# A macaron block on one core: the second FFN's routing as a table of pieces beside the attention's end, with transposes by transfers

## The chip, the cores and the metric

The kernel runs on one core of one Trainium2 chip. The metric is the device time of one execution in microseconds; the figure shown for a kernel is the median of its runs. The engines are called PE (matmuls; PEld is its weight loads), DVE, ACT, POOL and SP, as the profile calls them. "L814" is line 814 of the kernel before.

## The reference

The input x has 2 batches of 4096 tokens with 512 features, in float32. Three steps each add to x:

- x = x + 0.5 FFN(layernorm(x))
- x = x + attention(layernorm(x))
- x = x + 0.5 FFN(layernorm(x)), with the same FFN weights as in the first step

The FFN routes every token to 64 slots. A hidden layer of 256 (exact gelu) gives 64 logits, the 8 largest are kept, and a softmax over these gives the token's weights alpha. Each slot's input is the alpha-weighted mean of all tokens, so the whole sequence has to be routed before the slots are updated. A recurrent cell (GRU) updates the slots, and the output of a token is its alpha times the new slot values, projected:

```
h = gelu(concat(x, slot_mean) @ w1.T + b1)
alpha = softmax over the top 8 of (h @ w2.T + b2) / (|tau| + 0.1)
slot_input = sum over t of alpha[t] * x[t];   slots = GRU(slot_input / sum of alpha, slots)
out = (alpha @ (slots @ wv.T + bv)) @ wo.T + bo
```

The attention is a linear one with a delta rule, in 16 heads of 32: q and k are normalised, a and b are sigmoids of projections, and a state of 32x32 per head runs over the tokens:

```
state = a * state + (b * (v - state @ k)) outer k;   y = state @ q
out = (rmsnorm(y) * g_norm * silu(x @ Wg)) @ Wo
```

## The kernel before, in words

The tokens are cut into 32 blocks of 128 positions, with both batches in one block (tile shapes carry NB = 2). Projections that need more than float16 precision are done as three float16 matmuls, from a high half and a low half of each operand (`mm3`, L127 to L130).

**The first FFN's routing** (`ffn_a_phase`, L309, called with "a") works in groups of 1, 4, ..., 4, 3 and 1 blocks. Every stage of a group is a generator with a start and an end on a common scale (PA, L1095), and `run_merged` (L60) merges them by due time. The stages: `a_load` brings x; `a_stats` (L355) takes mean and variance; `a_norm` (L368) writes the normalised tokens, casts them to the high half on ACT (L383), subtracts on POOL for the low half (L385), transposes both halves by 16 PE transposes a block into PSUM (L394) and copies them out, the high one on ACT (L397), the low one on DVE (L399); `a_hidden` (L402) does the hidden layer and the logits (L421); `a_topk` (L425) the top 8 and the weights; `a_slots` (L463) sums tokens into slots in one PSUM bank that stays open for the whole phase. Beside it the attention's weights are prepared: `split16` (L175) makes a high half on ACT and a low half on DVE. `gru` (L509) then updates the slots.

**The attention** (L647) is a software pipeline over the blocks. `PIPE` (L1097) is a table of words such as "prep.6": in each period k the generator of that stage for block k + 6 takes one step. One period handles one block, by stages of up to eight neighbouring blocks; its order is the order of every engine's queue (`run_pipe`, L75). `prep` (L781) adds the first FFN's output (`ffn_b`, L486), stores x1d, normalises, transposes the float32 block by four PE transposes for each batch (L814), casts to the high half on ACT (L816) and subtracts for the low half on DVE (L818). `qkproj` and `vgproj` project; `post` normalises q and k; `kk`, `dec`, `solve` make a triangular system and invert it on DVE; `chain` (L1000) carries the state over four chunks of the block; `tail` (L1056) applies gate, norm and output projection (L1080), adds x1 (L1083) and stores the block into x2d. The PSUM pool of the projections has three buffers, shared by the projections, by `prep`'s output of the FFN and by the tail.

**The second FFN** (`ffn_a_phase` with "c", L644) starts after the attention's pools are closed, so its first instructions wait for all of these. It loads x2d on SP (L602), keeps the last 12 blocks in SBUF (KEEP, L37), routes as the first one does, runs the recurrent cell, and then (`after_c`, L624) makes the output block by block (L641) and stores it.

Transfers issued by SP and ACT stand in these engines' instruction queues in program order. Pools allocated over freed memory wait for the whole of the pool that was there.

Of the kernel before, what the change touches and what calls it, by code (L numbers as in the profile page):

```python
# [19 lines left out]
P = 128  # L20
# [14 lines left out]
HEAD, TAIL = 1, 1  # L35
CFG = {"a": dict(XT=7, XN=2, XH=10), "c": dict(XT=4, XN=2, XH=11)}
KEEP = 12  # L37
F3A, F3X, F3L = 4, 11, 8
# [14 lines left out]
def split_blocks(n):  # L53

    cuts = [0] + list(range(HEAD, n - TAIL, GB)) + [n - TAIL, n]
    cuts = sorted(set(cuts))
    return [(a, b - a) for a, b in zip(cuts, cuts[1:])]
# [17 lines left out]
def run_pipe(tc, stages, n):  # L75


    order = []
    for w in PIPE.split():
        w, _, m = w.partition("*")  # L80
        name, lead = w.split(".")
        order += [(name, int(lead))] * int(m or 1)
    live = {}
    with tc.manual_schedule():
        for k in range(-max(lead for _, lead in order), n):
            for name, lead in order:
                t = k + lead
                if 0 <= t < n:
                    if (name, t) not in live:
                        live[name, t] = stages[name](t)  # L90
                    next(live[name, t], None)
# [3 lines left out]
def tile_macaron(  # L95
# [82 lines left out]

    isc1 = cp.tile([P, 1], F32, tag="isc1", name="isc1")
# [3 lines left out]
    aw = aw_es.enter_context(tc.tile_pool(name="aw", bufs=1))  # L183
    W = {}
    for n_, cols, dt in (("wqh", NQ, F16), ("wql", NQ, F16), ("wgh", 2 * D, F16), ("wgl", 2 * D, F16),
                         ("wo", D, F32)):
        W[n_] = aw.tile([P, KC, cols], dt, tag=n_, name=n_)
# [43 lines left out]
    def setup_gh(gp, big, ppj):  # L231
# [3 lines left out]
        whht = big.tile([P, KC, 3 * D], F32, tag="big", name="whht")  # L235
        for k in range(KC):
            nc.sync.dma_start(whht[:, k], whh[k * P:(k + 1) * P])
# [3 lines left out]
        nc.sync.dma_start(bsum, bhh.rearrange("(k p) -> p k", p=P))  # L241
        V.tensor_tensor(bsum[:, 0:8], bsum[:, 0:8], bihn[:, 0:8], ALU.add)
        ghb = gp.tile([P, 12, NS], F32, tag="ghb", name="ghbs")
        yield 0.1
        for g in range(12):
            pg = ppj.tile([P, NS], F32, tag="tr", name=f"pgh{g}")
            for k in range(KC):
                nc.tensor.matmul(pg, whht[:, k, g * P:(g + 1) * P], hsT[:, k], start=(k == 0), stop=(k == KC - 1))
            V.tensor_scalar(ghb[:, g], pg, bsum[:, g:g + 1], None, ALU.add)
            yield 0.1 + 0.9 * (g + 1) / 12  # L250
        nc.sync.dma_start(ghd, ghb)

    def setup_attention(gp, big, ppj):
# [5 lines left out]
        yield 0.1  # L259
        scales(gp, ppj, [s1[:, :, 0:2 * D], s1[:, :, 2 * D:]], scA[:, 0:2], iscA[:, 0:2], "wq")  # L260
        yield 0.3
        for k in range(KC):
            for s, i in ((slice(0, 2 * D), 0), (slice(2 * D, NQ), 1)):
                o = [W[n_][:, k, s] for n_ in ("wqh", "wql")]
                if i == 0:

                    o = [a.rearrange("p (q e g) -> p q g e", g=NG, e=C) for a in o]
                    src = s1[:, k, s].rearrange("p (q g e) -> p q g e", g=NG, e=C)
                    for g in range(NG):
                        split16(*(a[:, :, g] for a in o), src[:, :, g], scA[:, i:i + 1])  # L270
                else:
                    split16(*o, s1[:, k, s], scA[:, i:i + 1])
            yield 0.3 + 0.05 * (k + 1)
# [3 lines left out]
        yield 0.5  # L277
        scales(gp, ppj, [s2[:, :, 0:D], s2[:, :, D:]], scA[:, 2:4], iscA[:, 2:4], "wg")
        yield 0.7
        for k in range(KC):  # L280
            for i in range(2):
                s = slice(i * D, (i + 1) * D)
                split16(W["wgh"][:, k, s], W["wgl"][:, k, s], s2[:, k, s], scA[:, 2 + i:3 + i])
            yield 0.7 + 0.03 * (k + 1)
        gt = gp.tile([P, KC], F32, tag="gt", name="gt")
        nc.sync.dma_start(gt, gnorm.rearrange("(k p) -> p k", p=P))
        s3 = big.tile([P, KC, D], F32, tag="big", name="wo32")
        for k in range(KC):
            nc.sync.dma_start(s3[:, k], wo_a[k * P:(k + 1) * P])
        for k in range(KC):  # L290
            nc.scalar.mul(W["wo"][:, k], s3[:, k], gt[:, k:k + 1])
            yield 0.85 + 0.03 * (k + 1)
# [16 lines left out]
    def ffn_a_phase(load, adst, nm, extra, before=None, after=None):  # L309

        with tc.tile_pool(name=f"sl{nm}", bufs=1, space=PSUM) as slp, tc.tile_pool(name=f"gp{nm}", bufs=1) as gp:
            sl = slp.tile([P, KC, NB, NS], F32, tag="sl", name=f"sl{nm}")
            wacc = gp.tile([P, GB * NB, NS], F32, tag="wacc", name=f"wacc{nm}")
            gw = {}
            with tc.tile_pool(name=f"f{nm}", bufs=2) as wp, tc.tile_pool(name=f"fs{nm}", bufs=2) as sm, \
                    tc.tile_pool(name=f"ft{nm}", bufs=3, space=PSUM) as ptr, \
                    tc.tile_pool(name=f"fp{nm}", bufs=2, space=PSUM) as ppj, \
                    tc.tile_pool(name=f"fl{nm}", bufs=2, space=PSUM) as ppl:
                groups = split_blocks(NBLK)
                ng = len(groups)  # L320
                pools = (wp, sm, ptr, ppj, ppl)
                st = [dict() for _ in range(ng)]
                items = []
                for g, (b0, n) in enumerate(groups):
                    args = (st[g], nm, g, (b0, n), pools)
                    t0, t1 = b0 / GB, (b0 + n) / GB
                    items += [
# [840 lines left out]
```

## Time and profile before

| what | us |
|---|---|
| median of 3 runs | 2353.59 |
| lowest and highest run | 2349.47, 2361.57 |
| the profiled execution, its own time | 2342.8 |
| its span | 2341.0 |
| one attention period | 51.4 |

| stretch of the span, us | what runs there |
|---|---|
| 0 to 300 | first routing, preparing weights, recurrent cell |
| 300 to 468 | the attention's pipeline fills |
| 468 to 1959 | 29 periods of the attention |
| 1959 to 2004 | the last chain, the last tails |
| 2004 to 2250 | second routing |
| 2250 to 2341 | recurrent cell, output |

How to read it: the page gives each engine's busy time over the whole span, and the span in 40 slices of 58.5 us with the busy share in tenths, so that a 9 is 90% or more. Matmuls are pipelined and their ends are modelled, so that the busy time of PE is not its time at peak: where a price of PE is needed, the time from one start to the next is used. The views by stretch give, for each stretch, the busy time of every engine, the granted clock, and the share of the 16 DMA engines. A line of a group of instructions gives its line in the code, engine and operation, the tile written and the tiles read, the shapes and the count; then the busy time, the mean in ns, and the idle time before it with what ended it.

### The profile page before, as it was taken

The numbers are of one execution on the slowest core, as the hardware profiler recorded it, in microseconds if no ns is written. First come the engines' busy times: TensorE is split into PE (matmuls) and PEld (weight loads), VectorE is DVE, ScalarE is ACT, GpSimd is POOL, SyncE is SP. The second block draws the span as 40 slices with busy tenths as digits, with TensorE's granted clock in tenths as the row PEclk, the third lists the DMA queues.
The fourth block names the chain that finished last, engine by engine and source line by source line (L and its number), as shares of the span: only waits on it lengthen the run. The fifth ranks groups of instructions, "written<-read, shape, count | busy, mean of one in ns | idle before, by whom it ended". The sixth has DMA issues, their size and how long they took to land. (4 is left out here: it accounts for less than half of the span.)

```text
span 2341.0 us, 101047 instructions
## 1 busy us (share of the span) xinstructions
PE 2100.5 (90%) x44989; PEld 1585.4 (68%) x44989; DVE 1911.3 (82%) x4876; ACT 1148.9 (49%) x1957; POOL 808.5 (35%) x750
## 2 busy tenths in 40 slices
PE   5878878999999999999999999999999976588886
PEld 5767757767777676777767677777667754377774
DVE  7898538988888888888889888888888886489656
ACT  4677445544445444444545444554444421367631
POOL 2333114433334343333434333444333441134300
PEclk9898989999999999999999999999999988799997
DMA  6332323344443344343334444344444332630049
GB/s 212 123 127 91 96 87 129 119 133 130 142 134 126 123 136 132 128 150 121 126 124 139 128 136 148 120 127 132 135 128 146 102 97 70 219 110 29 2 149 368
DMA packets 176516, 302.75 MB, mean 129 GB/s; under 512 B 27984, under 2 KB 73552, under 8 KB 176080
## 3 DMA queue, kind: packets, MB, share of 16 engines
q1 hardware_dynamic: 161728, 256.45, 32.9%
q10 hardware_dynamic: 14352, 39.85, 5.2%
q8 instruction: 352, 5.77, 1.2%
q14 instruction: 84, 0.69, 0.1%
HBM read 189.23 MB, written 107.00 MB: 127 GB/s over the span
## 5 line engine op out<-in xcount | busy, mean ns | idle before, releaser
L1080 PE MATMUL apo<-wo,Gt 128*128 128x512 f32 x512 | 279.1, 630 | 24.5 <-DVE x1r L1083 24.5
L128 PE MATMUL pv<-xTh,wgh 128*128 128x256 f16 x1024 | 282.1, 275 | 0.0
L129 PE MATMUL pv<-xTh,wgl 128*128 128x256 f16 x1024 | 280.2, 274 | 0.1
L130 PE MATMUL pv<-xTl,wgh 128*128 128x256 f16 x1024 | 280.3, 274 | 0.0
L1014 POOL TENSOR_TENSOR ps<-ST,AC 128x256 f32<-128x256 f32 x128 | 105.5, 824 | 442.4 <-DVE ST L1038 442.4
L128 PE MATMUL pq<-wqh,xTh 128*128 128x384 f16 (+1 forms) x768 | 242.8, 316 | 1.5 <-issue 0.8
L129 PE MATMUL pq<-wqh,xTl 128*128 128x384 f16 (+1 forms) x768 | 240.9, 314 | 0.2 <-DVE xTl L818 0.2
L130 PE MATMUL pq<-wql,xTh 128*128 128x384 f16 (+1 forms) x768 | 240.7, 313 | 0.0
L862 POOL TENSOR_TENSOR qk<-qk,rn 128x512 f32<-128x512 f32 x128 | 137.6, 1075 | 231.7 <-issue 106.7
L836 ACT ACTIVATE qk<-pq,iscA 128x384 f32<-128x384 f32 (+1 forms) x192 | 105.4, 549 | 162.5 <-PE pq L130 139.5
L980 POOL TENSOR_TENSOR KQ<-KQ,Ax 128x512 f32<-128x512 f32 x128 | 168.4, 1315 | 0.4 <-PE pa L959 0.4
L764 DVE TENSOR_TENSOR tmp<-N,MT 128x256 f32<-128x256 f32 (+7 forms) x384 | 161.2, 426 | 5.6
L758 DVE TENSOR_TENSOR tmp<-N,U 128x256 f32<-128x256 f32 (+7 forms) x384 | 164.0, 434 | 1.4
L838 ACT ACTIVATE sq<-pq,iscA 128x384 f32<-128x384 f32 (+1 forms) x192 | 164.7, 858 | 0.0
L1018 PEld LDWEIGHTS pc<-KQ,S 32*32 32x32 f32 x8192 | 123.2, 106 | 50.6 <-ACT Y L1044 31.0
L760 DVE TENSOR_REDUCE MT<-tmp 128x32 f32<-128x256 f32 (+7 forms) x384 | 153.8, 407 | 0.0
L959 PE MATMUL pa<-KQ 32*32 32x64 f32 x8192 | 143.6, 217 | 11.2 <-ACT KQ L872 4.9
L1018 PE MATMUL pc<-KQ,S 32*32 32x64 f32 x8192 | 142.8, 217 | 9.5 <-DVE S L1040 4.9
L959 PEld LDWEIGHTS pa<-KQ 32*32 32x32 f32 x8192 | 121.7, 105 | 37.9 <-issue 14.9
L1035 PEld LDWEIGHTS pc<-X,u 32*32 32x32 f32 x8192 | 120.7, 105 | 38.6 <-issue 21.9
L1035 PE MATMUL pc<-X,u 32*32 32x64 f32 x8192 | 141.9, 216 | 5.2 <-ACT u L1032 3.7
L917 ACT ACTIVATE vg<-pv,iscA 128x512 f32<-128x512 f32 x128 | 88.1, 688 | 96.7 <-PE pv L130 88.7
(304 smaller groups left out, 5760.3 us busy)
## 6 DMA issues: line engine op xcount, KB each, us to landing
d<-a0d ACTq DMA_DIRECT2D x32, 528.0 KB
Ax<-a0d ACTq DMA_DIRECT2D x32, 528.0 KB
xt<-in_x_dram SPq DMA_DIRECT2D x32, 512.0 KB
x<-in_x_dram SPq DMA_DIRECT2D x64, 256.0 KB
x1d<-x SPq DMA_DIRECT2D x64, 256.0 KB
vtd<-vg SPq DMA_DIRECT2D x64, 256.0 KB
kd<-qk SPq DMA_DIRECT2D x64, 256.0 KB
XK<-kd SPq DMA_DIRECT2D x256, 64.0 KB
```

The source lines that it names most:

```text
L128: nc.tensor.matmul(po, lh, rh, start=start, stop=False, skip_group_check=True)
L129: nc.tensor.matmul(po, ll, rh, start=False, stop=False, skip_group_check=True)
L130: nc.tensor.matmul(po, lh, rl, start=False, stop=stop, skip_group_check=True)
L758: V.tensor_tensor(tv, vw(f, o10 + j0, [[C, n], [0, h], [1, ni]]), vw(U, ou + j0 * 17, [[0, n], [16, h], [1, ni]]), ALU.mult)
L760: yield lambda tv=tv, j0=j0: V.tensor_reduce(vw(mt, n * j0, [[1, n], [n, h]]), tv, AX.X, ALU.add)
L764: V.tensor_tensor(tv, vw(f, o11 + r0 * C, [[C, h], [0, n], [1, nk]]), vw(mt, 0, [[0, h], [n, n], [1, nk]]), ALU.mult)
L838: nc.scalar.activation(sq[:, f0:f1].rearrange("p (q g e) -> p q e g", g=NG, e=C), pq[:, 0:f1 - f0].rearrange("p (q e g) -> p q e g", g=NG, ...
L959: nc.tensor.matmul(pa[s, m], KQ[s, 0, c, b, g], KQ[s, :, c, b, g], start=(m == 0), stop=True, skip_group_check=True, tile_position=(32 * q ...
L980: nc.gpsimd.tensor_tensor(kc, kc, bass.AP(Ax.tensor, Ax[:, :, c].offset, [list(a[0]), [1, 2], list(a[1]), [1, C]]), ALU.mult)
L1018: nc.tensor.matmul(pcv[s, b, g, 0:2 * C], S[s, b, g], KQ[s, :, c, b, g], start=(g == 0), stop=False, skip_group_check=True, tile_position=tp)
L1035: nc.tensor.matmul(pcv[s, b, g, C:3 * C], u[s, b, g], d["X"][s, :, m], start=False, stop=True, skip_group_check=True, tile_position=tp)
L1080: nc.tensor.matmul(po, Gt[:, k, b], wo[:, k], start=(k == 0), stop=(k == KC - 1))
```

## The change

Four things are changed.

- **The second routing becomes a table of its own.** `ffn_a_phase` is cut into `route_open` and `route_close`; the stages yield at each small step; `ROUTE` is a table of words as PIPE is, with one period for a group of blocks, and the groups of the second FFN are 1, 3, 4, ..., 4, 3, 1. The logits are a stage of their own. `pieces` walks a table as a generator. The first FFN's routing still goes by due times (`merged`).
- **It is begun beside the attention's last three periods.** The attention's pools are split into an early and a late set. After the last step of any stage before the last four (vload, chain, tload, tail) the early set is closed, `open_c` opens the second routing's pools in that memory, and the routing's pieces are taken in proportion to the attention's until its period 0 has been done (AHEAD = 1.0). The x2 loads are issued by ACT. Pools wait by tile, not by pool (`reuse_waits="tile"`).
- **Token halves become feature-major by transposing transfers** (`dma_start_transpose`, on SP): in `prep` the block is cast to a high half and subtracted to a low half first, and both are transposed by transfers from SBUF to SBUF; in the second routing likewise. The first routing keeps its PE transposes.
- **Around it:** PIPE is written anew; the tail's and `prep`'s PSUM tiles move to a pool of one buffer (`ppo`) and the projections keep two; `setup_attention` splits weights by two ACT passes and a POOL subtraction (`split16p`) in finer steps; the normalised tokens overwrite the loaded ones except for kept blocks; buffer counts change (CFG, KEEP, F3X, F3L).

```diff
-CFG = {"a": dict(XT=7, XN=2, XH=10), "c": dict(XT=4, XN=2, XH=11)}
-KEEP = 12
-F3A, F3X, F3L = 4, 11, 8
+HEAD, TAIL = (1, 4), (4, 1)
+CFG = {"a": dict(XT=7, XH=9), "c": dict(XT=6, XH=8)}
+KEEP = 11
+AHEAD = 1.0
+F3A, F3X, F3L = 4, 12, 9
...
+def pieces(stages, n, table, extra=()):
...
+    for k in range(-max(lead for _, lead in order), n):
+        for e, (name, lead) in enumerate(order):
+            others(k + e / len(order))
+            t = k + lead
+            if 0 <= t < n:
+                if (name, t) not in live:
+                    live[name, t] = stages[name](t)
+                next(live[name, t], None)
+                yield k + (e + 1) / len(order)
+    others(n + 1)
...
+    def split16p(hi, lo, src, s):
+        nc.scalar.mul(src, src, s)
+        nc.scalar.copy(hi, src)
+        nc.gpsimd.tensor_tensor(lo, src, hi, ALU.subtract)
...
+    def route_open(nm, load, adst, extra, side):
...
+        ptr, ppj, ppl = (pool(fs, *a, space=PSUM) for a in (("ft", 3 if nm == "a" else 1), ("fp", 2), ("fl", 1)))
...
+    def a_norm(d, nm, g, pools):
...
             nc.scalar.copy(xh, xn)
+            yield
+            if nm == "a":
+                nc.gpsimd.tensor_tensor(xl, xn, xh, ALU.subtract)
...
+            else:
+                nc.sync.dma_start_transpose(xTh, flat(xh))
+                yield
+                nc.gpsimd.tensor_tensor(xl, xn, xh, ALU.subtract)
+                yield
+                nc.sync.dma_start_transpose(xTl, flat(xl))
+                yield
...
+    def load_x2(wp, t):
+        if t >= NBLK - KEEP:
+            xt = keep[t] = pk["xk"].tile([P, NB, D], F32, tag=f"x2_{t}", name=f"kx2_{t}")
+            xn = pk["xk"].tile([P, NB, D], F32, tag="xn", name=f"kxn{t}", bufs=2)
+        else:
+            xt = xn = wp.tile([P, NB, D], F32, tag="xt", name=f"xt2_{t}", bufs=CFG["c"]["XT"])
+        nc.scalar.dma_start(xt, x2d[t * P:(t + 1) * P])
+        return xt, xn
...
+    def open_c():
+        aw_es.close()
+        pk["ak"] = kp.enter_context(tc.tile_pool(name="ak", bufs=1, side="right", reuse_waits="tile")).tile(
+            [P, NBLK, NB, P], F16, tag="ak", name="ak")
+        pk["r"] = route_open("c", load_x2, alpha_keep, extra_c, "right")
+        return pieces(*pk["r"]["args"])
...
-        ppj = pool("a1p", 3, space=PSUM)
+        ppo = pool("a1o", 1, space=PSUM)
+        ppj = epool("a1p", 2, space=PSUM)
...
-                pt = ptr.tile([P, KC, P], F32, tag="tr", name=f"apt{t}_{b}")
-                for k in range(KC):
-                    nc.tensor.transpose(pt[:, k], xs[b][:, k * P:(k + 1) * P], ident)
-                yield
-                nc.scalar.copy(xTh[:, :, b], pt)
-                yield
-                V.tensor_tensor(xTl[:, :, b], pt, xTh[:, :, b], ALU.subtract)
+                xh = we.tile([P, D], F16, tag="xh", name=f"xh{t}_{b}", bufs=2)
+                nc.scalar.copy(xh, xs[b])
+                yield
+                nc.sync.dma_start_transpose(xTh[:, :, b], xh)
+                yield
+                xl = we.tile([P, D], F16, tag="xl", name=f"xl{t}_{b}", bufs=2)
+                V.tensor_tensor(xl, xs[b], xh, ALU.subtract)
+                yield
+                nc.sync.dma_start_transpose(xTl[:, :, b], xl)
                 yield
...
-        run_pipe(tc, stages, NBLK)
+        late = ("vload", "chain", "tload", "tail")
+        drain = NBLK - min(lead for name, lead in leads(PIPE) if name not in late)
+        rest = None
+        with tc.manual_schedule():
+            for now in pieces(stages, NBLK, PIPE):
+                if now >= drain and rest is None:
+                    ee.close()
+                    rest = open_c()
+                    at = next(rest)
+                    first = at
+                if rest is not None:
+                    while at < first + (AHEAD - first) * (now - drain) / (NBLK - drain):
+                        at = next(rest)
+    return rest
```

The new table of the routing:

```
ROUTE = """
    hid.2*2 topk.1*3 hid.2 load.4 topk.1 slots.0 topk.1*3 norm.2 topk.1 norm.2 stats.3 hid.2 norm.2 stats.3 topk.1 hid.2*3
    logit.2 stats.3*2 norm.2 hid.2 stats.3 norm.2 topk.1 hid.2 topk.1 hid.2 stats.3 norm.2 topk.1*2 hid.2*3 topk.1 logit.2
    hid.2 topk.1*2 norm.3 slots.1*4 norm.3 load.4 norm.3 slots.1*2 hid.2 slots.1 norm.3*2 slots.1 hid.2 norm.3*2 hid.2
    slots.1 norm.3*3 hid.2 norm.3*2 hid.2 topk.1 norm.3 stats.4 slots.1*2 stats.4 slots.1 hid.2 load.4 hid.2*2 logit.2
    norm.3*3 stats.4*2 norm.3 logit.2 slots.1 load.4 topk.2 hid.3 norm.3 slots.1 hid.3 topk.2*2 slots.1
"""
```

## The prediction

> **What bounds the kernel now.** I read four views in this order: the page (engine shares and slices), busy time by stretches, the waits of TensorE in the middle, and single rows where a price is needed. The page first.
>
> ```profile
> span 2341.0 us, 101047 instructions
> ...
> PE 2100.5 (90%) x44989; PEld 1585.4 (68%) x44989; DVE 1911.3 (82%) x4876; ACT 1148.9 (49%) x1957; POOL 808.5 (35%) x750
> ...
> PE   5878878999999999999999999999999976588886
> ...
> DVE  7898538988888888888889888888888886489656
> ```
>
> PE is at 9 only in the middle; both ends are lower, so the 90% is no statement about the ends. The stretches say where they are (columns: length, then busy us of PE, weight loads, DVE, ACT, POOL, granted clock, DMA share, GB/s).
>
> ```profile
> 468.00:1959.00 1491.00, 1435.61 (x36251) 1036.70 (x36249) 1302.73 (x3277) 700.62 (x1278) 579.49 (x582) 0.99 0.40 129
> 1959.00:2004.00 45.00, 30.80 (x738) 18.12 (x738) 11.12 (x22) 4.30 (x10) 3.83 (x5) 0.79 0.16 54
> 2004.00:2052.00 48.00, 26.02 (x237) 21.68 (x238) 28.40 (x73) 20.64 (x26) 11.60 (x7) 0.72 0.77 283
> 2052.00:2250.00 198.00, 165.75 (x2132) 147.35 (x2131) 156.56 (x455) 136.58 (x190) 71.77 (x39) 0.94 0.10 34
> 2250.00:2341.00 91.00, 63.29 (x280) 45.84 (x277) 54.51 (x108) 16.35 (x41) 0.00 (x0) 0.82 0.89 332
> ```
>
> I set the cuts. The last triangular solve ends at about 1959, and one attention period is 51.4 us (the same store of vtd is issued at 1009.69 and 1061.08), so 468 lies 29 periods earlier. In those 29 periods PE is busy 96%: the attention is bound by PE's work in order. From 1959 to 2004 the last chain and two tails run one after another, and DVE works 11 of 45 us. From 2004 the second routing starts cold: DVE 28 of 48 us, at a clock of 0.72. From 2052 to 2250 no engine is full (PE 84%, DVE 79%, ACT 69%). After 2250 the stores end last (DMA share 0.89).
>
> The seam at 2004 is a chain, seen in the timeline:
>
> ```profile
> 1999.21 0.32 SPq L1054 DMA_DIRECT2D x1r<-x1d  x1
> 2001.80 0.75 DVE L1083 SCALAR_TENSOR_TENSOR x1r<-apo,rms,x1r 128x512 f32<-128x512 f32 x1 [4.62 <-DMA x1r<-x1d]
> 2002.58 0.32 SPq L1085 DMA_DIRECT2D x2d<-x1r  x1
> 2004.76 0.52 POOL L460 MEMSET waccc<- 128x512 f32 x1 [15.07 <-DMA x2d<-x1r]
> 2004.76 3.28 SPq L602 DMA_DIRECT2D xt<-x2d  x4
> ```
>
> The routing's first load waits for the attention's very last store, though it reads block 0, stored 1500 us earlier; its first DVE instruction comes at 2012.05.
>
> **The change, part by part.** All sums are against the profiled execution, 2342.8 us (span 2341.0 and 1.8 around it); the median shown is 2353.59, 10.8 longer, and I move the result by that.
>
> *Attention's transposes.* Eight float32 transposes a period (L814) leave PE. Their busy time (272 ns each) overlaps, so I take the time until PE's next instruction starts:
>
> ```profile
> 1024.49 0.60 PE L814 MATMUL apt<-ident,x 128*128 128x128 f32 x4
> 1025.02 1.09 PE L1035 MATMUL pc<-X,u 32*32 32x64 f32 x64
> ...
> 1053.50 0.60 PE L814 MATMUL apt<-ident,x 128*128 128x128 f32 x4
> 1053.94 0.29 PE L128 MATMUL pq<-wqh,xTh 128*128 128x288 f16 x1
> ```
>
> 0.53 + 0.44 = 0.97 us a period. The copy and the subtraction remain, one on ACT (0.59) and one on DVE (0.68), now from SBUF. PE also waits:
>
> ```profile
> PE apo L1080 <- DVE x1r L1083: 20.4, 23, 1.8
> ```
>
> that is 0.85 us in each of some 24 periods. The new order and the tail's own PSUM bank could remove it, or add to it: one bank is now shared by the tail's sums, its two projections and prep's two, so each waits until DVE or ACT has read the last. I take no change in waits: 0.84 x 32 = -27 us, rounding 0.97 down for the first periods, which are not PE-bound. Bounds: 0.97 + 0.85 over 32 is -58; above, see the transfers.
>
> *Transposing transfers.* Four a period of 128 KB, 64 in the second routing of 256 KB, all on SP. No row of before has one. From below: the final stores move 379 GB/s (2300 to 2341), so 256 KB takes 0.7 us and 128 KB half of it. From above: the 161,728 packets of the main queue take 32.9% of 16 engines' 2341 us, 76 ns each; as rows of 256 bytes, 256 KB is 1024 packets, 4.9 us, and 128 KB 2.45 us. I take 1.5 and 0.75 us, nearer the lower end since most bytes here run near it, and a latency of 2.6 us as the plain load above (1999.21 to 2001.80). Counted in the new table, the last low half is issued 0.09 period, 4.5 us, before the projection that reads it, so 2.6 us is covered; where it is not, PE stops with all that stands behind. Each SP transfer also waits for ACT's or DVE's half, and behind it stand the kd and vtd stores and the XK loads, 0.3 to 2.4 us to issue each; DMA is 40% busy. Price if uncovered: 1 us a period is 32 us.
>
> *Second routing and drain.* 512 PE transposes, 32 ACT copies and 32 DVE copies go:
>
> ```profile
> L394 PE MATMUL fptc<-ident,xlc 128*128 128x128 f16 x256 | 31.6, 229 | 11.9 <-POOL xlc L385 11.9
> L394 PE MATMUL fptc<-ident,xhc 128*128 128x128 f16 x256 | 26.7, 225 | 20.9 <-ACT xhc L383 20.8
> L397 ACT COPY fxThc<-fptc 128x1024 f16<-128x1024 f16 x32 | 32.4, 1011 | 5.7 <-PE fptc L394 5.6
> L399 DVE COPY fxTlc<-fptc 128x1024 f16<-128x1024 f16 x32 | 21.7, 677 | 15.2 <-PE fptc L394 15.2
> ```
>
> From 2004 to 2250 that leaves PE 191.8 - 58.3 = 133.5, ACT 157.2 - 32.4 = 124.8, DVE 185.0 - 21.7 = 163.3 us: DVE is next. With the drain's own 11.1 it has 174 us of work between 1959 and the recurrent cell, and now all of it may overlap, since 11 blocks are normalised and 8 hidden beside the last chain and tails. At 85% full that is 205, and 10 for the last group's chain of logits, top-8 and slots (17 us at the end of before, part of it counted): 215 against 291, -76 us. Bounds of the filling: DVE's 79% of before gives 220 + 17 = 237, -54; its 97% between 100 and 200 us gives 180 + 10, -101. The chain's DVE steps now queue behind routing's (0.7 us each, up to 2.5 beside POOL); that is inside these ends. The x2 loads move to ACT's queue, where the chain's u and Y copies stand behind a load that waits for freed memory: at most the solve's lag, 5 us.
>
> *The first routing and setup.* 24 splits leave DVE (16 of 967 ns and 8 of 859, 22.4 us), ACT does each twice (852 and 720 ns more, 19.4 us), POOL subtracts (from 2.16 us per 1024 elements: 17.3 us). DVE is 97% busy there, ACT 75%: -5 us, between -15 and +10 (POOL beside DVE costs DVE time). The seam at 265 to 300, where waits go by tile, and the fill: -3, between -12 and +10, since prep's latency now has a transfer in it. The ending: one block more to load, 1.4 us, hidden or not: 0, between -10 and +5.
>
> Sum: -27 - 76 - 5 - 3 = -111. 2342.8 - 111 = 2232; against the median 2353.59 - 111 = **2243**.
>
> **A rule against it, and one for it.** No run here shows either. The Trainium skill, "VectorE: DVE Perf Modes", section "The three transpose paths", gives 1309 ns for a 128x128 block by DMA and 390 ns by TensorE; if eight blocks of a half queued up so, 64 halves would take 670 us, and the sum would be far slower than before. "Advanced Engine Details and Errata", section "X-Bar Transpose (TRN2)", calls such transfers as fast as ordinary ones at 350 to 400 GB/s; by that a half is 0.7 us and the sum stands.
>
> **The rivals.** (1) Forecast, 2243, own range 2195 to 2290, chance 0.53. (2) The overlap pays but the attention does not: the low halves land late behind XK loads (up to three of 0.55 to 2.4 us on SP) or the shared bank stops PE. At 1.6 us a period the 0.97 turns into +0.65, +21 instead of -27: 2291, chance 0.20. For: the one bank and 4.5 us of slack. Against: the tail's wait of 0.85 can go. (3) It doesn't do what it says: the begun routing cannot start since its memory is freed too late, or its pieces only lengthen the drain; then only DVE's copies count, -22 instead of -76: 2297, chance 0.08. (4) Slower: transposing transfers at 4.9 us a half. 64 halves take 314, with 25 to start 339 instead of 215, +124; in the attention two low and high halves in a row (2.45 each) miss the 4.5 us by some 2.5 with latency, +80: 2447. It decides from 64t + 25 = 215 + 111, t = 4.7 us a half, even if the attention is spared; chance 0.14. The rest, 0.05, is gains and losses that cancel.
>
> Faster by over 0.5% (about what a measurement of this kernel can tell from no change) is (1), (2) and most of (3): 0.80; within 0.06; slower 0.14. The range, 2190 to 2350, takes in the first three cases and leaves (4) out.
>
> **What would show it.** The period between equal stores falls to about 50.5 us; PE's wait for x1r stays under 1 us a period; no large wait of PE for a transfer into xTh or xTl; the 48 us gap of low DVE after the last store is gone; last store of x2d to the recurrent cell falls from 248 us to about 150. It is wrong if SP is seen waiting long behind a transpose, if a half lands over 4 us after issue, or if the drain grows by more than the 30 us that it takes from later.

## The result, and the profile after

The changed kernel takes 2431.1 us (median of 4 runs, 2419.34 to 2448.22) against 2354.99 us of before (4 runs, 2349.47 to 2361.57): ratio 1.0328, 95% interval 1.0256 to 1.0399. It is slower by 76 us; the forecast was 2243 and the range ended at 2350. The profiled execution of after took 2436.47 us with a span of 2434.7. Its page:

```profile
span 2434.7 us, 99970 instructions
...
PE 2098.8 (86%) x44221; PEld 1558.7 (64%) x44221; DVE 1891.1 (78%) x4816; ACT 1207.1 (50%) x2017; POOL 808.8 (33%) x778
...
PE   5787877889999999999999899999999996668775
...
DVE  7968545878888888878888788888888888366646
...
DMA packets 313873, 336.78 MB, mean 138 GB/s; under 512 B 165216, under 2 KB 210784, under 8 KB 313440
```

TensorE (PE) executes 768 matmuls fewer than before and is busy for about the same time, 2098.8 us against 2100.5; the count of packets under 512 bytes is 165216, where before has 27984:

```profile
DMA packets 176516, 302.75 MB, mean 129 GB/s; under 512 B 27984, under 2 KB 73552, under 8 KB 176080
```

The transposing transfers move 33.5 MB, and the trace's own packet records show them as rows of 256 bytes.

To find the loss I cut both profiled executions at the same four instructions: the first recurrent cell's first matmul (pw), the first and the last triangular solve (the DVE instruction that writes TT), and the second recurrent cell's first matmul. All kernels of this study, in us of their profiled executions, with the median time and its ratio to the kernel before, measured beside it:

| kernel | start to first cell | to first solve | first to last solve | to second cell | to the end | median | ratio [95%] |
|---|---|---|---|---|---|---|---|
| before | 273.9 | 132.5 | 1551.4 | 292.3 | 90.9 | 2354.99 | 1 |
| after | 291.5 | 143.8 | 1628.3 | 280.6 | 90.5 | 2431.10 | 1.0328 [1.0256, 1.0399] |
| attn_pe | 292.6 | 129.8 | 1518.7 | 279.1 | 90.9 | 2319.49 | 0.9829 [0.9800, 0.9859] |
| rout_pe | 294.8 | 146.0 | 1617.7 | 344.2 | 91.3 | 2495.49 | 1.0574 [1.0548, 1.0601] |
| both_pe | 294.2 | 129.8 | 1518.7 | 345.0 | 90.9 | 2378.38 | 1.0076 [1.0049, 1.0103] |
| attn_plain | 294.3 | 143.8 | 1680.6 | 276.8 | 92.4 | 2507.73 | 1.0601 [1.0546, 1.0656] |
| pe_oldsplit | 280.0 | 129.7 | 1515.9 | 270.6 | 91.0 | 2297.41 | 0.9747 [0.9721, 0.9774] |
| pe_dummy | 295.5 | 135.8 | 1620.9 | 276.8 | 89.6 | 2418.28 | 1.0261 [1.0243, 1.0280] |
| dummy_plain | 291.7 | 135.5 | 1511.1 | 281.4 | 91.1 | 2310.38 | 0.9797 [0.9774, 0.9819] |
| attn_none | 291.9 | 131.3 | 1499.5 | 274.1 | 90.9 | 2288.64 | 0.9716 [0.9694, 0.9738] |
| pe_late | 292.4 | 133.1 | 1519.2 | 265.5 | 90.2 | 2298.04 | 0.9743 [0.9715, 0.9770] |
| pe_mix | 293.5 | 130.8 | 1519.1 | 292.5 | 91.0 | 2328.71 | 0.9883 [0.9865, 0.9901] |
| pe_seq | 293.9 | 131.1 | 1515.3 | 296.1 | 90.9 | 2328.20 | 0.9895 [0.9854, 0.9937] |
| rout_none | 291.2 | 131.4 | 1518.7 | 251.9 | 90.5 | 2285.92 | 0.9710 [0.9687, 0.9734] |
| late_oldsplit | 281.9 | 132.6 | 1516.7 | 266.9 | 90.8 | 2288.62 | 0.9719 [0.9697, 0.9741] |
| best_fl2 | 285.5 | 130.4 | 1517.6 | 268.8 | 90.6 | 2292.68 | 0.9720 [0.9692, 0.9748] |
| best_xn | 284.4 | 131.4 | 1517.8 | 260.9 | 93.0 | 2290.60 | 0.9724 [0.9701, 0.9747] |
| best_xn_fl2 | 286.2 | 130.2 | 1516.9 | 262.8 | 90.2 | 2291.65 | 0.9725 [0.9701, 0.9748] |

Of the four runs of attn_plain one, 2539.68, was in a slower state of the chip, and the other three have a median of 2502.05. Rows with the same code in a stretch differ there by up to 4 us in the start and in the attention (1515.3 to 1519.2 with TensorE transposing) and by up to 11 us in the stretch to the second cell (270.6 to 281.4); smaller differences are not read. From before to after, the start is longer by 17.6, the fill (from the first cell to the first solve) by 11.3, the attention by 76.9; the second routing is shorter by 11.7, hardly more than such a difference. With the ending this adds up to 93.7 us, as the two spans do; the medians differ by 76, since the profiled execution of before was 12 us under its median and that of after 5 above.

**The attention.** The stretch from first to last solve, of before and of after (columns as in the prediction's table: length, busy us of PE, weight loads, DVE, ACT, POOL, granted clock, DMA share, GB/s):

```profile
406.40:1957.80 1551.40, 1492.78 (x37849) 1080.26 (x37847) 1357.99 (x3420) 734.55 (x1338) 604.22 (x606) 0.99 0.40 128
```

```profile
435.30:2063.60 1628.30, 1509.25 (x37698) 1077.65 (x37696) 1377.02 (x3419) 798.38 (x1391) 586.14 (x606) 0.97 0.55 131
```

PE has less to execute and is busy 16 us longer, at a clock of 0.97 instead of 0.99; beyond that it is idle 119 us instead of 59. What ended the idle time, between 600 and 1700 us of after:

```profile
PE pc L1148 <- issue: 27.3, 18, 2.6
PE pc L1141 <- issue: 11.3, 4, 9.1
PE pq L159 <- DMA xTl<-xl: 6.8, 4, 1.9
PE pq L159 <- issue: 4.1, 2, 2.4
```

The wait for x1r that the prediction showed is gone. In its place stands "issue", time in which nothing that the profile shows kept TensorE waiting: 73.8 us from first to last solve, where before has 8.6. The wait for a transposed half is small. One such place in after, by the timeline:

```profile
1035.23 0.98 PE L1148 MATMUL pc<-X,u 32*32 32x64 f32 x54
...
1035.49 4.51 SPq L930 DMA_TRANSPOSE xTl<-xl  x1
...
1037.24 0.38 PE L1148 MATMUL pc<-X,u 32*32 32x64 f32 x10 [1.03 <-issue]
...
1040.89 0.50 PE L159 MATMUL pq<-wqh,xTl 128*128 128x384 f16 x1 [2.43 <-issue]
...
1041.18 0.53 PE L160 MATMUL pq<-wql,xTh 128*128 128x384 f16 x1
```

TensorE stops in the middle of 64 equal small matmuls, after 54 of them, with every operand there, while SP issues a transposing transfer; it stops again at 1038.46, for 2.43 us, and then its matmuls take 0.50 to 0.53 us where the same form took 0.34 before the gap: the trace's clock records show a granted clock of 0.50 from 1039.2 to 1046.0. So the idle time is paid for twice, the second time by the clock. The second stop is no wait for the low half that is under way, since the last rows of that transfer move until 1041.8, after TensorE has gone on.

**The second routing.** After, in stretches of about 50 us from the last solve on:

```profile
2063.60:2110.00 46.40, 27.95 (x732) 18.78 (x733) 17.67 (x40) 6.58 (x14) 7.92 (x8) 0.68 0.32 92
2110.00:2160.00 50.00, 32.14 (x190) 21.75 (x190) 24.73 (x81) 23.56 (x29) 13.53 (x8) 0.75 0.70 153
2160.00:2210.00 50.00, 40.17 (x419) 34.10 (x419) 35.06 (x121) 29.18 (x42) 19.18 (x10) 0.86 1.02 169
2210.00:2260.00 50.00, 36.60 (x443) 32.34 (x441) 33.73 (x117) 29.97 (x43) 19.42 (x10) 0.94 1.06 172
2260.00:2310.00 50.00, 40.80 (x485) 35.91 (x484) 33.22 (x97) 34.17 (x48) 19.77 (x10) 0.91 0.81 164
```

In the first 96 us DVE is busy 42: the seam of low DVE is not gone; it was 39 of 93 us before, so nothing was gained there. From 2160 to 2260 all 16 DMA engines are taken (share 1.02 and 1.06) at 169 to 172 GB/s, and TensorE waits for them:

```profile
PE fphc L160 <- DMA fxTlc<-xlc: 22.7, 16, 3.8
PE fphc L158 <- DMA fxThc<-xhc: 18.5, 9, 4.1
PE fphc L158 <- ACT hTc L472: 10.8, 9, 4.1
```

### The profile page after: what moved, and what is told of

Same layout as the page of the kernel before. It is cut to its first block, busy times and chain, and to the rows that moved or that the text cites. A ratio compares the mean times of both kernels' runs of the same rounds, so it can differ in the third digit from the quotient of the medians.

```text
span 2434.7 us, 99970 instructions
## 1 busy us (share of the span) xinstructions
PE 2098.8 (86%) x44221; PEld 1558.7 (64%) x44221; DVE 1891.1 (78%) x4816; ACT 1207.1 (50%) x2017; POOL 808.8 (33%) x778
## 2 busy tenths in 40 slices
DMA packets 313873, 336.78 MB, mean 138 GB/s; under 512 B 165216, under 2 KB 210784, under 8 KB 313440
## 4 chain that ended last, share of the span: by engine, by line
PE 61%; DMA 7%; DVE 6%; issue 4%; ACT 2%; POOL 1%; ACTq 0%; SPq 0%; DVEq 0%; POOLq 0%
PE apo L1193 10%; PE pc L1148 6%; PE pc L1131 5%; PE pa L1071 5%; PE pq L158 5%; PE pv L158 4%; PE pq L159 4%; PE pq L160 4%; PE pv L159 4%; PE pv L160 4%; PE pc L1141 3%; DMA fxTlc<-xlc 3%; DMA xTl<-xl 3%; PE kqt L981 2%; PE fpoa L556 1%
## 5 line engine op out<-in xcount | busy, mean ns | idle before, releaser
L159 PE MATMUL pq<-wqh,xTl 128*128 128x384 f16 (+1 forms) x768 | 250.7, 326 | 17.1 <-DMA xTl<-xl 13.0
L160 PE MATMUL pq<-wql,xTh 128*128 128x384 f16 (+1 forms) x768 | 250.9, 327 | 8.0 <-issue 7.9
L974 POOL TENSOR_TENSOR qk<-qk,rn 128x512 f32<-128x512 f32 x128 | 150.5, 1177 | 310.3 <-issue 229.7
L1097 POOL TENSOR_TENSOR X<-XK,Dx 128x256 f32<-128x256 f32 x128 | 98.6, 771 | 322.3 <-PE pc L1148 208.6
L1093 POOL TENSOR_TENSOR KQ<-KQ,Ax 128x512 f32<-128x512 f32 x128 | 153.1, 1196 | 123.9 <-PE pa L1071 121.2
L1148 PE MATMUL pc<-X,u 32*32 32x64 f32 x8192 | 152.6, 220 | 41.0 <-issue 39.1
L1148 PEld LDWEIGHTS pc<-X,u 32*32 32x32 f32 x8192 | 127.4, 107 | 94.1 <-issue 68.0
L1127 POOL TENSOR_TENSOR ps<-ST,AC 128x256 f32<-128x256 f32 x128 | 87.5, 684 | 266.2 <-DVE ST L1151 234.1
L1131 PE MATMUL pc<-KQ,S 32*32 32x64 f32 x8192 | 152.6, 224 | 21.3 <-DVE S L1153 14.2
L1151 DVE TENSOR_TENSOR ST<-pc,ps 128x256 f32<-128x256 f32 x128 | 52.2, 408 | 151.0 <-PE pc L1148 122.1
L1145 ACT COPY u<-pc 128x256 f32<-128x256 f32 x128 | 48.5, 379 | 223.0 <-PE pc L1141 150.1
```

Of the source, the lines that this page charges most:

```text
L159: nc.tensor.matmul(po, ll, rh, start=False, stop=False, skip_group_check=True)
L160: nc.tensor.matmul(po, lh, rl, start=False, stop=stop, skip_group_check=True)
L974: nc.gpsimd.tensor_tensor(qw, qw, bc(rw, 2, C), ALU.mult)
L1093: nc.gpsimd.tensor_tensor(kc, kc, bass.AP(Ax.tensor, Ax[:, :, c].offset, [list(a[0]), [1, 2], list(a[1]), [1, C]]), ALU.mult)
L1131: nc.tensor.matmul(pcv[s, b, g, 0:2 * C], S[s, b, g], KQ[s, :, c, b, g], start=(g == 0), stop=False, skip_group_check=True, tile_position=tp)
L1148: nc.tensor.matmul(pcv[s, b, g, C:3 * C], u[s, b, g], d["X"][s, :, m], start=False, stop=True, skip_group_check=True, tile_position=tp)
```

## The experiments

Unless a diff says otherwise, each starts from the changed kernel; "attn_pe" is the base of most.

**attn_pe, rout_pe, both_pe: which of the two places loses?** The attention's part goes back (the order of the pieces stays, the casts' places hold the transposes; the pieces' `yield` lines and the arguments at "..." are left out here):

```diff
-                xh = we.tile([P, D], F16, tag="xh", ...)
-                nc.scalar.copy(xh, xs[b])
-                nc.sync.dma_start_transpose(xTh[:, :, b], xh)
-                xl = we.tile([P, D], F16, tag="xl", ...)
-                V.tensor_tensor(xl, xs[b], xh, ALU.subtract)
-                nc.sync.dma_start_transpose(xTl[:, :, b], xl)
+                pt = ptr.tile([P, KC, P], F32, tag="tr", ...)
+                for k in range(KC):
+                    nc.tensor.transpose(pt[:, k], xs[b][:, k * P:(k + 1) * P], ident)
+                nc.scalar.copy(xTh[:, :, b], pt)
+                V.tensor_tensor(xTl[:, :, b], pt, xTh[:, :, b], ALU.subtract)
```

and in rout_pe the second routing's (16 float16 transposes a block, an ACT and a DVE copy, through the one bank; the copy of alpha moves up beside its transposes, since all use that bank). both_pe does both.

> Only the attention goes back to eight float32 TensorE transposes a period, in the new order and with the tail's own bank; the second routing keeps its transposing transfers. Theory (the transposing transfers stall TensorE): the gaps put down to issue go, first to last triangular solve falls from 1628 us to between 1545 and 1570, the time from 2431 to about 2360. Rival (the new order of the pieces, or one PSUM bank shared by five users, costs the time): periods stay at 52 us and above, and the time stays above 2415.

> Only the second routing goes back to TensorE transposes, with one PSUM bank for them; the attention keeps its transposing transfers. Theory (the second routing is bound by DMA, which the transposing transfers fill): last triangular solve to second recurrent cell falls from 281 us to about 240, the time to about 2390. Rival (the routing begun early does not gain, whatever carries the transposes; or one bank for the transposes is the next bound): that stretch stays at 280 us or grows to 300, and the time is 2430 or more.

> Neither stage has transposing transfers; new tables, early second routing, new setup splits and the tail's own bank stay. Theory (the transfers are what costs): both gains add, about 2320. Rival (new order, bank or early routing cost): 2400 or more.

Measured: attn_pe 2319.49, below the kernel before, with 1518.7 us from first to last solve. The idle time of PE put down to issue falls from 73.8 to 2.5 us there, and the clock is back at 0.99:

```profile
422.30:1941.00 1518.70, 1490.35 (x37926) 1081.11 (x37924) 1374.28 (x3418) 790.16 (x1391) 585.52 (x606) 0.99 0.39 131
```

So the attention's loss is that of its transposing transfers, and the rival (new order, shared bank) falls: the new order with its bank, TensorE transposing as before, is 33 us faster than the old. For the second routing my theory fell: with TensorE transposes that stretch grows to 344 us instead of falling to 240. That is more than the 300 us of the rival. both_pe, 2378.38, lies between its two expectations. In both_pe PE waits there for the cast and the subtraction right before its transposes:

```profile
PE fptc L454 <- ACT xhc L432: 23.3, 16, 4.4
PE fptc L454 <- POOL xlc L449: 20.5, 16, 1.6
```

That the table leaves no distance between them, or that there is one bank where before had three: these two were not told apart.

**attn_plain: is it the transposing?** `dma_start_transpose(xTh[:, :, b], xh)` becomes `dma_start(xTh[:, :, b], xh.rearrange(...))`, and the same for xTl.

> The attention's transfers stay where they are, with the same bytes, queue and waits, in rows of 256 bytes, but copy and do not transpose, so the projections read blocks that are not transposed. If it is the transposing that costs, the time falls to about 2360 as in attn_pe; if it is a small transfer of 256-byte rows at this place and its waits, it stays at about 2430.

Measured 2507.73, slower still. But the mechanism differs, as the waits of PE between 600 and 1700 show:

```profile
PE pq L159 <- DMA xTl<-xl: 101.8, 19, 8.7
```

Here PE waits for the half itself, up to 8.7 us, which the transposing transfer did not make it do; "issue" is down to 0.9 us in the whole stretch. Neither expectation was right, since the experiment mixed a latency with an interference.

**pe_dummy and dummy_plain: the interference alone.** attn_pe with four transfers a period that nobody reads, once transposing and once plain:

```diff
+        dsrc = we.tile([P, D], F16, tag="dsrc", name="dsrc")
...
+                dd = we.tile([P, KC, P], F16, tag="dd", name=f"dh{t}_{b}", bufs=2)
+                nc.sync.dma_start_transpose(dd, dsrc)
...
```

(the same once more behind the subtraction; in dummy_plain the last line is a `dma_start` of `dsrc.rearrange("p (k i) -> p k i", k=KC)`).

> As attn_pe, with four more transposing transfers a period from a constant tile into tiles that nobody reads, at the places and on the queue where the changed kernel has its own; it computes the same. Theory (transposing transfers hold up the DMA engines and with them TensorE's instructions): first to last triangular solve grows from 1519 to between 1580 and 1620 us and gaps put down to issue come back; the time is about 2400. Rival (the loss came from PE and ACT waiting for the halves themselves): the stretch stays within 10 us of 1519.

> As pe_dummy, but the four added transfers a period copy their 128 KB in rows of 256 bytes and do not transpose; nobody reads them. Theory (transposing holds up a DMA engine for microseconds, rows of 256 bytes do not): first to last triangular solve is within 15 us of 1519, against 1621 in pe_dummy, and the time is about 2325. Rival (the number of small packets is what costs): 1600 or more, about 2410.

Measured: the transposing ones cost 102 us between the solves, the plain ones nothing (1511.1). First pe_dummy, then dummy_plain:

```profile
431.30:2052.20 1620.90, 1517.52 (x37925) 1094.43 (x37922) 1375.90 (x3419) 793.89 (x1391) 584.80 (x606) 0.98 0.57 132
```

```profile
427.30:1938.30 1511.00, 1485.14 (x37914) 1077.93 (x37912) 1380.22 (x3418) 789.89 (x1391) 583.74 (x604) 0.99 0.43 141
```

Both moved the same 16.8 MB more than attn_pe, but not in the same rows. dummy_plain was meant to copy rows of 256 bytes; its tile `dd` is contiguous, and the packet records show rows of 1024 bytes, a quarter as many packets. So it does not by itself rule out that the number of small packets costs. attn_plain, whose copies are in 256-byte rows, is set beside it in the packet records below.

Only the transposing ones raise the DMA share by 0.18 (the plain ones by 0.04), make PE's own instructions busy 27 us longer and bring back the gaps (pe_dummy, waits of PE between 600 and 1700; dummy_plain has none over the view's limit):

```profile
PE pc L1153 <- issue: 28.9, 22, 2.7
PE pc L1146 <- issue: 11.0, 4, 7.5
PE pc L1136 <- issue: 8.7, 12, 1.6
```

Issue is 73.8 us from first to last solve in pe_dummy, 71 more than in attn_pe; with the 27 us this is 98 of the 102 us. The packet records of the traces say how, between first and last solve:

```
                                         attn_pe  after  pe_dummy  dummy_plain  attn_plain
256-byte packets                               0  58368     58368            0       58368
2048-byte packets over 1 us                   12    446       409            2           0
4-byte packets over 1 us                       0    397       534            0           0
16-KB instruction packets over 3 us            0     13         4            0           0
longest instruction packet, us               2.9   10.0       9.2          2.3         2.7
over 8 us between two instruction packets     10     31        38            8          29
```

Beside transposing transfers some hundreds of the packets of others that take 84 ns (2048 bytes) or 9 ns (4 bytes) in the median take over a microsecond, and some of the instruction queue's packets of 16 KB, 1.0 to 1.1 us in the median, take 3 to 10 us. In attn_plain, with as many 256-byte rows, none of them does: it is the transposing, not the rows. (The last line of the table tells little, since attn_plain, whose TensorE stands still for its halves, has 29 there.) Of the 41 gaps over 0.3 us put down to issue in after, 14 (27.3 of 73.0 us) end 1.3 to 1.6 us after an instruction packet of 16 KB ended, the second stop of the timeline above among them (a packet of 3.2 us, up to 1039.59). That fits a TensorE out of instructions. The other gaps, most of them 1 to 2.5 us in the middle of L1148 and some 2 us after the low half's issue, have no instruction packet right before them in the records; that they have the same cause is argued, not shown. That transposing transfers bring them is shown by pe_dummy against dummy_plain and attn_plain, which have 0.4 and 0.9 us of issue in the stretch.

**attn_none: what could the transposes' removal bring at best?** The cast and the subtraction write xTh and xTl directly, with nothing transposed.

> As attn_pe, but the attention's blocks are not transposed at all: ACT casts the normalised rows straight into xTh and DVE subtracts, so neither TensorE nor a transfer does that work and the projections read blocks that are not transposed. It gives the most that taking the transposes off TensorE could bring. If TensorE's order of work is the bound, as the prediction has it, 0.97 us for each of 31 periods: first to last triangular solve from 1519 to about 1489 us, time about 2290. Rival (DVE, 90% busy in that stretch, or the chain binds as soon as TensorE has room): 1510 or more.

```profile
423.10:1922.60 1499.50, 1469.23 (x37698) 1058.40 (x37697) 1379.79 (x3418) 790.02 (x1391) 585.43 (x606) 0.99 0.40 132
```

1499.5: 19 us less than attn_pe, 0.62 us a period where 0.97 was forecast, midway between the two expectations (1489 and 1510). TensorE is busy 98% of it, so it binds, and of each period's 0.97 us about a third goes elsewhere.

**pe_oldsplit: the longer start.** `split16p` becomes `split16` in the setup's splits of the attention's weights.

> As attn_pe, with the setup's splits as before (one ACT instruction and one DVE instruction each, none on GpSimd). Theory (the longer start comes from the new splits): first recurrent cell falls from 292.6 to about 275 us and the time from 2319 to about 2302. Rival (it comes from normalising in place, which holds the loaded blocks longer, or from the single bank for the logits): it stays at 290 or above, the time at 2319, or goes up since DVE has 22 us more to do.

280.0 instead of 292.6: the new splits cost 12.6 us of the longer start. They do take work from DVE, as the stretch from 100 to 200 us shows, first of after, then of pe_oldsplit:

```profile
100.00:200.00 100.00, 80.76 (x1036) 72.03 (x1036) 80.28 (x215) 75.23 (x123) 47.07 (x37) 0.91 0.36 114
```

```profile
100.00:200.00 100.00, 78.66 (x994) 70.20 (x993) 96.17 (x238) 69.43 (x101) 33.88 (x17) 0.91 0.33 104
```

With the new splits DVE has 16 us less to do in these 100 us, and the kernel is slower for it: DVE was nearly full there, and yet a gain could not be read from that. One wait comes and goes with the new splits. The first routing's low half is subtracted on POOL, which now has the splits too, and PE waits for it between 20 and 293 us; first of attn_pe, then of pe_oldsplit:

```profile
PE fpta L440 <- POOL xla L435: 9.5, 7, 2.1
```

```profile
PE fpta L440 <- POOL xla L435: 2.8, 3, 1.2
```

In before this wait is 1.4 us, in after 9.0. It makes up about half of the 12.6 us at most; that it does is not shown, and through which waits the rest is lost was not settled.

**best_fl2, best_xn, best_xn_fl2: the rest of the longer start.** From late_oldsplit (below), two banks for the first routing's logits (`("fl", 2 ...)`), a tile of its own for the normalised rows (`return xt, wp.tile(..., tag="xn", bufs=2)`), and both.

> As late_oldsplit, with two PSUM banks instead of one for the first routing's logits, as before the change. If the single bank makes the start longer, the first recurrent cell falls from 281.9 to about 275 us; if not, it stays within 2 us.

> As late_oldsplit, but the first routing normalises into tiles of its own (two buffers, as before the change) and not in place, so that loaded blocks are freed sooner. If holding the blocks makes the start longer (DVE waited 11 us for loads of x in the changed kernel), the first recurrent cell falls from 281.9 to about 275 us; if not, it stays within 2 us.

> best_xn and best_fl2 together. If both edits count, the first recurrent cell falls to the 273.9 us of before and the time from 2289 to about 2280; if neither, 281 us and 2289.

285.5, 284.4 and 286.2 against 281.9: neither is the cause. Some 6 to 8 us of the start stay unexplained; the new order and fineness of the setup's pieces is a cause left, not tested.

**pe_seq and pe_late: what is the early start worth?** pe_seq runs the routing's pieces behind the attention in one order with it; pe_late sets `AHEAD = -10.0`.

> As attn_pe, with the whole second routing in order behind the attention's last instruction on every engine, as one order with it, so that nothing overlaps. (In pe_late the compiler's scheduler merged the two orders itself, so it did not show this.) Theory (the early start as the change places it gains little): last triangular solve to second recurrent cell 279 becomes 280 to 295. Rival (the overlap is worth the 40 us and more of the drain): 315 or more.

> As attn_pe, with the second routing begun only behind the attention's last piece. Theory (in the drain almost none of the routing ran, and what follows is bound by DMA): last triangular solve to second recurrent cell grows from 279 by 5 to 20 us. Rival (the overlap is worth the 40 to 60 us that were forecast, and something else took them back): it grows by 40 us or more.

pe_seq: 296.1 against 279.1, so the early start as the change has it is worth some 17 us, of which up to 11 may be the drift named above. pe_late was to show the same and did not, since the two orders, no longer tied, were merged by the compiler's scheduler: its first transposing transfer is issued at 1960.6, ahead of the attention's last four stores; in attn_pe it comes at 1979.7. It gives 265.5, 13.6 less than attn_pe, part or most of which may be that drift too.

**rout_none and pe_mix: what binds the second routing?** rout_none lets the hidden layer read xh and xl as they are; pe_mix moves the high halves alone to TensorE.

> As attn_pe, but in the second routing the halves are not transposed at all: the hidden layer reads xh and xl as they stand, with no transfer, no TensorE transpose and no copy. If the transfers are what binds that stretch, DVE is next, as the prediction has it: 279 falls to 215 to 230 us. Rival (the order of the pieces and its waits bind, with transfers only in their cover): 255 or more.

> As attn_pe, and in the second routing the high halves go by TensorE and an ACT copy, through the one bank, the low halves by transposing transfers. Theory (that stretch is bound by the transfers, 64 halves in some 220 us): half of them fewer takes it from 279 to about 245, the time to about 2285. Rival (with TensorE transposes the one bank and ACT bind, as in both_pe): between 290 and 345, the time 2330 to 2378.

Without any transposition the stretch is 251.9, just under the rival's line: transposing costs 27 us of the stretch (19 to 30 against the other rows with the early start and transfers), and 37 us more lie between 251.9 and the forecast's 215. rout_none from its last solve on:

```profile
1941.30:1990.00 48.70, 30.36 (x744) 20.50 (x745) 18.41 (x41) 8.41 (x16) 7.90 (x8) 0.68 0.27 90
1990.00:2040.00 50.00, 35.22 (x226) 25.09 (x224) 31.14 (x97) 27.94 (x34) 16.66 (x10) 0.81 0.44 167
2040.00:2090.00 50.00, 44.23 (x566) 39.73 (x565) 43.19 (x132) 35.27 (x52) 22.78 (x11) 0.97 0.31 105
2090.00:2140.00 50.00, 42.58 (x541) 38.65 (x540) 42.15 (x146) 34.59 (x50) 23.25 (x13) 1.00 0.28 98
2140.00:2193.30 53.30, 41.15 (x531) 37.12 (x531) 30.54 (x105) 32.91 (x51) 16.04 (x12) 0.84 0.21 65
```

DVE is 85% full from 2040 to 2140, the share that I had assumed for the whole; in the first 99 us it is 50%, in the last 53 us 57%. pe_mix brings the DMA share of the stretch from 0.74 to 0.48 and is slower, 292.5, in its rival's range: there PE waits 29.2 us for the cast before its transposes.

```profile
PE fptc L451 <- ACT xhc L432: 29.2, 19, 6.7
```

So neither way of transposing fits the order that the table has for it, and "bound by DMA" was half the truth.

**late_oldsplit: the pieces that gain, together.**

> pe_late and pe_oldsplit together: TensorE transposes in the attention, setup splits as before, the second routing with its transposing transfers merged into the attention's end by the scheduler. If the two gains are separate, 2319 - 22 - 21 = about 2276. If they were partly the same drift of the last stretch, about 2290.

2288.62, ratio 0.9719 [0.9697, 0.9741]: 66 us under before. The two gains did not add, as its second expectation said: the last stretch is 266.9, against 270.6 in pe_oldsplit, so most of pe_late's gain there can be the same drift. Of the kernels that leave nothing out it is the fastest, level with its three variants: the change's new orders, early routing and tail bank, with TensorE transposing in the attention and the old splits.

## Why the prediction was wrong

The step that failed first is "Transposing transfers". It asked how long a transfer takes and whether it lands before it is read, and priced a miss as PE waiting for a half. Both answers were near enough: PE's wait for xTl is 8.3 us in the whole stretch. What it left out, and so put at nothing, is what a transposing transfer does to everything else: other packets take microseconds, TensorE stops for issue (73.8 us), and its granted clock falls (0.97 in the stretch, 0.99 before). No row of before could show that, and the bounds (0.7 to 4.9 us) bounded the wrong quantity. Attention: forecast -27, measured +76.9. By the runs: the new order and its bank -32.7 (attn_pe against before), the eight transposes off TensorE -19.2 (attn_none against attn_pe), the transfers +128.8 (after against attn_none). The first two, -52, lie inside the bounds of -58 that the step gave: its reading of what binds the stretch was right, and taking no change in waits was too careful, since the x1r wait did go. The fill (+11.3 against -3) is the same cause: attn_pe has 129.8 there, 2.7 under before.

"Second routing and drain": forecast -76, measured -11.7, outside its bounds of -54 to -101. The work left for DVE was right (161 us measured, 174 forecast), and it is the next bound in the middle; "at 85%" failed. Filling of an engine was taken from a full stretch and put on a stretch with a cold end, a chain and a last group. The early start was worth some 17 us, not the 45 us of the drain: the x2 loads on ACT's queue stand behind the chain's copies (in attn_pe the first goes out at 1947.8, the next at 1968.2 and 1977.7, each right behind a copy of u or Y or a square of the tail), and the cast before the first transposing transfer ends at 1979.7. The transposing then costs 27 us more. From the last store of x2d to the recurrent cell it takes 213 us (2131.3 to 2344.2) where about 150 was named as the mark.

"Setup": forecast -5 with an upper bound of +10, measured +17.6, of which the splits are 12.6. DVE at 97% was taken as the bound of that stretch; relieving it by 16 us made it longer. The ending (0 forecast, -0.4 measured) was right.

Of the rivals, (4) named the right side and nearly the right time, 2447, for the wrong reasons: it put +124 into the second routing by 4.9 us a half, where that stretch became shorter (64 halves were issued within 223 us, 3.5 us each at most), and +80 into the attention by halves that come late, where they come in time and TensorE stops for something else. Rival (2) had the sign of the attention's change, and about a quarter of its size. The marks "x1r wait under 1 us a period" and "no large wait on xTh or xTl" held in a kernel that got slower, so they could not tell; the period itself could (median 52.3 us between solves, 50.6 before; the 51.4 of the prediction is a single period), and SP's 4.5 us behind one transposing transfer was among the signs named.

The two rules weighed: The Trainium skill, "Advanced Engine Details and Errata", section "X-Bar Transpose (TRN2)", has transposing transfers as fast as ordinary ones. The runs disagree beside other traffic: the same bytes cost 102 us as transposes (pe_dummy) and none as copies in larger rows (dummy_plain); in the same 256-byte rows, from first to last solve, their packets took 139 us of the 16 DMA engines as transposes (pe_dummy) and 69 us as copies (attn_plain); and the DMA engines are full at 169 to 172 GB/s in the second routing. "VectorE: DVE Perf Modes", section "The three transpose paths", would give, as an estimate, 670 us for 64 halves of eight blocks one after another; they were issued within 223 us, so that figure does not hold for halves that follow each other.

## What to carry to other kernels

A transfer that "is hidden" still shares DMA engines with everything else, and with the instructions of the engine that binds: price a new kind of transfer by a kernel that issues it for nobody to read, beside a plain one of the same shape, before moving work to it, and look in the packet records whether the two have the same rows. Gaps named issue in the middle of a run of equal matmuls are the sign; look then at the packets of the instruction queue. And take the filling of an engine from a stretch like the one that it is applied to, cold ends included.

## What the runs showed of the hardware

Issuing a transposing transfer holds SP four times as long as a plain one of whole rows (1.26 us in the median for 128 KB of xTl, 0.32 us for x1r), and up to 5 us at its longest, for the 256 KB of the second routing up to 6.6 us. In after and in attn_plain (duration in ns, min/median/max):

```profile
L930 SPq DMA_TRANSPOSE xTl<-xl x64: 1189/1256/4960, 328.6 to 1936.6; - x64
```

```profile
L930 SPq DMA_DIRECT2D xTl<-xl x64: 594/642/3592, 330.7 to 1998.3; - x64
```

A plain copy of 128 KB from SBUF to SBUF in 256-byte rows lands later than the transposing one at the same place (PE waits 101.8 us for it in 19 periods of attn_plain, 6.8 us in 4 of after), though no other packet of the kinds in the table above is held up in attn_plain.
